# Layer 1 of a two-layer graph network on one core: steps around the norms and the values, paired output tiles, and mask copies on ScalarE

## The chip, the cores and the metric

The kernel runs on one core of a Trainium2 chip. The core has five engines that work side by side, each through its own queue of instructions in order: TensorE (PE, its weight loads shown as PEld), VectorE (DVE), ScalarE (ACT), GpSimd (POOL) and SyncE (SP), which here only issues DMAs. The metric is the time of one execution on the device in microseconds. A profile is one execution recorded instruction by instruction.

## The reference, cut to what matters

There are 32 graphs ("batches") of 512 nodes with 256 features and one 512 x 512 adjacency of zeros and ones each. Two layers follow each other, each with a graph part and a feed-forward part on a layer-normed input, both added to x. The change touches layer 1 alone (besides the adjacency masks of its first batch, which are made while layer 0 still runs).

```python
# layer 1, graph part: 4 heads of 64
h = einsum('bnd,hde->bhne', layernorm(x), W)
weight = mask * (e_src[..., :, None] + e_dst[..., None, :])   # adjacency is 0 or 1
attention = softmax(where(adj == 0, NEG, leaky_relu(weight)))
dst = einsum('bhij,bhje->bhie', attention, h) + bias
out = relu(dst) + h
x = x + (out - mean(out)) / sqrt(var(out) + 1e-6) * gamma + beta      # over each head
# layer 1, feed-forward part: 8 heads of 64, 64 slices
xn = layernorm(x)
fx, xm = xn @ W_fx.T + b_fx, xn @ W_x.T + b_x
sw = softmax((xm @ W_slice.T + b_slice) / temp)                # tokens to slices
st = einsum('bhnc,bhng->bhgc', fx, sw) / (sw.sum(2) + 1e-5)    # slice tokens
ot = hydra(st)            # two-way state-space mixer over the 64 slices
x = x + einsum('bhgc,bhng->bhnc', ot, sw) @ out_w.T + out_b
```

## The kernel before, in words

A batch lies in SBUF as four tiles of 128 nodes (NT = 4) by 256 features. Layer 0 runs first and takes about 2480 us; layer 1 is the generator function `layer1_plain`.

Layer 1 is two streams of Python generators. The stream `attentions` does, batch by batch, `prepare(b)` and `attention(b)`; the preparation of batch b + 1 is interleaved with the attention of batch b by `woven`, in the proportion of `TURNS - 4` to `STEPS`. The stream `mixer(g)` does the feed-forward part for a group of two batches (GB = 2): `slices` for each batch, `tokens`, `scan`, and `unslice` for each batch. Each `yield` in the mixer says how many steps of the attention stream it wants; these are multiplied by `PACE`, which is 1.04 x 2 x (TURNS + STEPS) / WANTED, so that the attention stream runs slightly ahead until `prepare` is stopped by `AHEAD_X = 5` buffers of x. The yields settle only in which order the program is written down: a scheduler then orders the instructions on each engine, with the written order as the priority. So a yield issues nothing by itself.

In `prepare(b)`, POOL gathers the four tiles of x with indirect DMAs (x<-x2s), which need the buffer of batch b - 5 stored. `masks(b)` loads the adjacency (ai), turns it into bf16 with a row sum and a sum of squares on ACT (a, ai), transposes it on PE into a PSUM tile (maskp) of tag "any" and copies that into the uint8 mask. `normed` takes mean and variance on DVE (stc, mvc), the power -0.5 on POOL (`deviation`: an add, then a pow, rsc), the product -mean x power on DVE (shiftc), and the scaling of the four tiles on ACT (hv serves as the buffer). `turned` transposes on PE (x3T). PE then makes hp, ACT takes from it the exponentials and ht, POOL adds the bias (hv<-ht), the source terms go through DRAM to be broadcast to all partitions (own), and DVE multiplies the values hv by their exponentials, one product for each tile.

In `attention(b)`, DVE makes the weights att = max(own, other) x mask for each tile and head, PE multiplies them with hv (avp, two heads side by side) and sums them (adp, four heads side by side). `norm` divides, adds, and normalizes over each head: a sum (mu), the difference, the square on ACT, a second sum, the power on POOL (mu<-mu,eps), and two products on DVE before x gets its sum.

In `slices(b)`, `normed` is used again (std, mvd, rsd, shiftd), the result is transposed (x4T), PE makes the logits of each tile (lgp), ACT the exponentials, DVE multiplies with the bias's exponential, sums, inverts and scales (sw: four operations for each tile), and PE makes yTp from all four tiles and transposes sw (swp). In `unslice(b)`, PE multiplies the transposed weights swT with v into outp and DVE adds each tile to x, which SP then stores.

The PSUM pool has four banks of tag "any"; maskp, x3T, x4T, hp, lgp, yTp, swp, outp and all of the mixer's products take turns in them. The other four banks have the tag "pv" and serve the attention's sums and their transposes.

Of the kernel before, what the change touches and what calls it, by code (L numbers as in the profile page):

```python
# [18 lines left out]
P = 128  # L19
N = 512  # L20
D = 256
NT = N // P
# [4 lines left out]
def deviation(nc, rs, var, eps):  # L27

    nc.gpsimd.tensor_add(rs, var, eps[:, 0:1].to_broadcast(rs.shape))
    nc.gpsimd.tensor_tensor(rs, rs, eps[:, 1:2].to_broadcast(rs.shape), ALU.pow)  # L30
# [819 lines left out]
def layer1_plain(tc, ident, eps, x2s, ranks, adj, w, out, over, ps):  # L850
# [21 lines left out]
    HE = HO + 1  # L872
    AP = AH // 2
    TURNS = AP * NT + 6
    STEPS = 15
    WANTED = 68
    AHEAD = 2
    ATT = 2 * (AHEAD + 2) + AP + 1
    HW = P // AH
# [6 lines left out]
    with ExitStack() as ctx:  # L886
# [11 lines left out]
        def psum(tag, name):  # L898
            return ps.tile([P, N], F32, tag=tag, name=name)
# [158 lines left out]
        def masks(b, bank="any"):  # L1058

            a, raw = [], []  # L1060

            def load(t):
                raw.append(se.tile([P, N], I32, tag="ai", name=f"ai{b}_{t}", bufs=2))
                nc.sync.dma_start(raw[t], adj[b, t * P : (t + 1) * P, :])

            def turn(t):
                pt = ps.tile([P, NT, P], BF16, tag=bank, name=f"maskp{b}_{t}")
                for j in range(NT):
                    nc.tensor.transpose(pt[:, j, :], a[t][:, j * P : (j + 1) * P], identb)
                nc.vector.tensor_copy(mask[:, :, t * P : (t + 1) * P], pt)  # L1070

            load(0)
            load(1)
            yield
            for t in range(NT):
                n = b * NT + t
                a.append(se.tile([P, N], BF16, tag="a", name=f"a{b}_{t}", bufs=3))
                nc.scalar.activation(a[t], raw[t], AF.Identity, accum_out=edges[:, 0, n : n + 1])
                nc.scalar.activation(raw[t], raw[t], AF.Square, accum_out=edges[:, 1, n : n + 1])
                if t + 2 < NT:  # L1080
                    load(t + 2)
                if t == 1:
                    mask = se.tile([P, NT, N], mybir.dt.uint8, tag="mask", name=f"mask{b}")
                    yield
                if t > 1:
                    turn(t - 2)
                    yield
            for t in range(NT - 2, NT):
                turn(t)
                yield  # L1090
            masked[b] = mask
# [11 lines left out]

        xs, ready, attended, stored = {}, {}, set(), set()

        def normed(xt, xn, name):

            mv = sb.tile([P, NT, 2], F32, tag="mv" + name[0], name=f"mv{name}")
            for t in range(NT):
                st = sb.tile([P, 6], F32, tag="st" + name[0], name=f"st{name}_{t}", bufs=4)  # L1110
                nc.vector.bn_stats(st, xt[:, t, :])
                nc.vector.bn_aggr(mv[:, t, :], st)
            rs = sb.tile([P, NT], F32, tag="rs" + name[0], name=f"rs{name}")
            deviation(nc, rs, mv[:, :, 1], eps)
            shift = sb.tile([P, NT], F32, tag="shift" + name[0], name=f"shift{name}")
            nc.vector.scalar_tensor_tensor(shift, mv[:, :, 0], -1.0, rs, ALU.mult, ALU.mult)
            for t in range(NT):
                nc.scalar.activation(xn[:, t, :], xt[:, t, :], AF.Identity, bias=shift[:, t : t + 1],
                                     scale=rs[:, t : t + 1])
# [13 lines left out]
        def prepare(b):  # L1133

            while b >= AHEAD_X and b - AHEAD_X not in stored:
                yield True
            xt = xs[b] = sb.tile([P, NT, D], F32, tag="x", name=f"x{b}", bufs=AHEAD_X)
            for t in range(NT):
                nc.gpsimd.indirect_dma_start(  # L1139
                    out=xt[:, t, :], out_offset=None, in_=x2s[b // SEG],  # L1140
                    in_offset=bass.IndirectOffsetOnAxis(
                        ap=ranks[:, b * NT + t : b * NT + t + 1].bitcast(U32), axis=0))

            hv = sb.tile([P, NT, AH, HE], F32, tag="hv", name=f"hv{b}")
            xn = hv.rearrange("p t h e -> p (t h e)")[:, : NT * D].rearrange("p (t d) -> p t d", t=NT)
            edged = masks(b) if b not in masked else range(3)
            for i, _ in enumerate(edged):
                if i < 3 or b not in masked:
                    yield
                if i == 2:  # L1150
                    normed(xt, xn, f"c{b}")
                    nc.gpsimd.tensor_add(xt, xt, beta.unsqueeze(1).to_broadcast([P, NT, D]))
                    yield
            mask = masked.pop(b)
            xnT = yield from turned(xn, "x3T", f"x3T{b}")
            yield


            ht = sb.tile([P, NT, AH * HO], F32, tag="ht", name=f"ht{b}")
            other = sb.tile([P, NT, AH], F32, tag="other", name=f"other{b}")  # L1160
            mine = sb.tile([P, AH, NT], F32, tag="mine", name=f"mine{b}")
            for t in range(NT):
                ph = psum("any", f"hp{b}_{t}")
                for c in range(DC):
                    nc.tensor.matmul(ph[:, : AH * (HO + 2)], xnT[:, c, t * P : (t + 1) * P], wa[:, c, :],  # L1165
                                     start=c == 0, stop=c == DC - 1)
                d = ph[:, AH * HO : AH * HO + AH]
                nc.scalar.activation(mine[:, :, t], ph[:, AH * (HO + 1) : AH * (HO + 2)], AF.Exp, scale=1.0 - SLOPE)
                nc.scalar.activation(hv[:, t, :, HO], d, AF.Exp)
                nc.scalar.activation(other[:, t, :], d, AF.Exp, scale=SLOPE - 1.0)  # L1170
                nc.scalar.copy(ht[:, t, :], ph[:, : AH * HO])
                yield

            nc.gpsimd.tensor_add(hv[:, :, :, :HO], ht.rearrange("p t (h e) -> p t h e", h=AH),
                                 abias.rearrange("p (h e) -> p h e", h=AH).unsqueeze(1).to_broadcast([P, NT, AH, HO]))
            yield
            pt = psum("any", f"minep{b}")
            nc.tensor.transpose(pt[: AH * NT, :P], mine.rearrange("p h t -> p (h t)"), ident)
            row = sb.tile([AH * NT, P], F32, tag="turned", name=f"turned{b}", bufs=1)
            nc.scalar.copy(row, pt[: AH * NT, :P])  # L1180
            own_row = dr.tile([AH, N], F32, tag="own", name=f"ownd{b}")
            nc.sync.dma_start(own_row.rearrange("h (t p) -> (h t) p", p=P), row)
            own = [wide("own", f"own{b}_{h}", AH + 2) for h in range(AH)]
            for h in range(AH):
                nc.sync.dma_start(own[h], own_row[h].partition_broadcast(P))
            for t in range(NT):
                nc.vector.tensor_mul(hv[:, t, :, :HO], hv[:, t, :, :HO], hv[:, t, :, HO:].to_broadcast([P, AH, HO]))
            ready[b] = mask, ht, hv, other, own
            yield
# [112 lines left out]
        def slices(b, j, yT, rn):  # L1302
# [3 lines left out]
                next(ahead)  # L1306
            xt = xs[b]
            xn = sb.tile([P, NT, D], F32, tag="xn", name=f"x4{b}", bufs=1)
            normed(xt, xn, f"d{b}")
            yield 5  # L1310
            xnT = yield from turned(xn, "x4T", f"x4T{b}", 1)
            nc.gpsimd.tensor_add(xt, xt, outb.unsqueeze(1).to_broadcast([P, NT, D]))
            sw = sb.tile([P, NT, DI], F32, tag="sw", name=f"sw{b}", bufs=1)
# [231 lines left out]

        def unslice(b, swT, v):
            xt = xs.pop(b)
            for t in range(NT):
                po = psum("any", f"outp{b}_{t}")
                for k in range(KC):  # L1550
                    nc.tensor.matmul(po[:, :D], swT[:, k, t * P : (t + 1) * P], v[:, k, :],  # L1551
                                     start=k == 0, stop=k == KC - 1)
                nc.vector.tensor_add(xt[:, t, :], xt[:, t, :], po[:, :D])
            nc.sync.dma_start(out[b].rearrange("(t p) d -> p t d", p=P), xt)
            stored.add(b)

        def mixer(g):
            uT = sb.tile([P, KC, GB * G], F32, tag="uT", name=f"uT{g}", bufs=1)
            yT = sb.tile([P, DC, H, GB, G], F32, tag="yT", name=f"yT{g}", bufs=1)
            rn = sb.tile([P, GB, KC], F32, tag="rn", name=f"rn{g}")  # L1560
            sws = []
            for j in range(GB):
                sws.append((yield from slices(g * GB + j, j, yT, rn)))
            yield 3
            tokens(g, yT, rn, uT)
            v = yield from scan(g, uT)
            yield 2
            for j in range(GB):
                unslice(g * GB + j, sws[j], v[:, j])
                yield 2  # L1570


# [651 lines left out]
```

## Time and profile before

| | |
|---|---|
| median of 3 runs | 4619.16 us (4616.48 to 4621.86) |
| the profiled execution's own time | 4623.49 us |
| its span, first to last instruction | 4621.6 us |
| granted PE clock in it | 0.951 |
| PE busy | 4067.9 us |
| DVE busy | 3379.1 us |
| ACT busy | 2291.7 us |
| POOL busy | 1729.5 us |
| DMA | 474.09 MB moved |

The page and the trace give busy time by engine, groups of instructions by line and tile with their mean duration, the idle time ahead of each group with what ended it, and an account of who waited for whom. In a group's row, "x128" is the count; after the bar stand the total busy time in us and the mean of one in ns; after the second bar the idle time of that engine just before these instructions, and the releasers. In a timeline the columns are start in us, duration in us, engine, line, operation, tiles, count, and in brackets the idle time before it with what ended it. In the account of waits a row gives the total in us, the number of times and the longest. A matmul of f32 operands stands in the trace as two instructions.

### The profile page before, as it was taken

The numbers are of one execution on the slowest core, as the hardware profiler recorded it, in microseconds if no ns is written. First come the engines' busy times: TensorE is split into PE (matmuls) and PEld (weight loads), VectorE is DVE, ScalarE is ACT, GpSimd is POOL, SyncE is SP. The second block draws the span as 40 slices with busy tenths as digits, with TensorE's granted clock in tenths as the row PEclk, the third lists the DMA queues.
The fourth block names the chain that finished last, engine by engine and source line by source line (L and its number), as shares of the span: only waits on it lengthen the run. The fifth ranks groups of instructions, "written<-read, shape, count | busy, mean of one in ns | idle before, by whom it ended". The sixth has DMA issues, their size and how long they took to land. (4 is left out here: it accounts for less than half of the span.)

```text
span 4621.6 us, 56127 instructions
## 1 busy us (share of the span) xinstructions
PE 4067.9 (88%) x19287; PEld 2525.4 (55%) x19287; DVE 3379.1 (73%) x7040; ACT 2291.7 (50%) x4756; POOL 1729.5 (37%) x2027
## 2 busy tenths in 40 slices
PE   5768898988988889888897899999999999999987
PEld 4545655656556566555554355555555555555555
DVE  6678778887788877777775777777787777777763
ACT  2344555545655556555564444545544454454432
POOL 2356444653435534353332223222323323332220
PEclk8889999999999999998998999999999999999998
DMA  5556433653436533374431111111111111111100
GB/s 125 172 158 214 164 127 126 198 178 124 136 118 198 177 129 112 99 263 145 141 115 48 53 46 56 51 48 44 44 54 49 56 56 53 47 54 56 40 14 15
DMA packets 235100, 474.09 MB, mean 103 GB/s; under 512 B 38299, under 2 KB 114075, under 8 KB 234804
## 3 DMA queue, kind: packets, MB, share of 16 engines
q0 software_dynamic: 80256, 282.38, 19.3%
q1 hardware_dynamic: 154548, 188.02, 13.3%
q8 instruction: 154, 2.52, 0.2%
q14 instruction: 142, 1.16, 0.1%
HBM read 413.16 MB, written 57.16 MB: 102 GB/s over the span
## 5 line engine op out<-in xcount | busy, mean ns | idle before, releaser
L609 PE MATMUL clsp<-xnT,wc 128*128 128x512 f32 x1024 | 512.1, 621 | 77.3 <-ACT cls L611 63.0
L609 PE MATMUL gatep<-xnT,wg 128*128 128x512 f32 x1024 | 497.7, 605 | 16.0 <-ACT gate L611 13.2
L638 PE MATMUL po<-wd,acc 128*128 128x256 f32 x2048 | 450.9, 381 | 0.4 <-DVE acc L627 0.3
L638 PEld LDWEIGHTS po<-wd,acc 128*128 128x128 f32 x2048 | 391.4, 191 | 65.9 <-issue 13.8
L422 PE MATMUL pm<-h,adj 128*128 128x257 f32 x1024 | 295.5, 435 | 136.3 <-DVE xs L640 67.3
L589 DVE SCALAR_TENSOR_TENSOR best<-rows,xs,best 128x1024 f32<-128x1024 f32 x212 | 276.1, 1305 | 165.4 <-ACT best L583 98.1
L623 DVE SCALAR_TENSOR_TENSOR acc<-past,fld,acc 128x512 f32<-128x512 f32 x448 | 351.1, 787 | 54.3 <-ACT past L622 45.5
L1198 DVE SCALAR_TENSOR_TENSOR att<-own,other,mask 128x512 f32<-128x512 f32 x512 | 378.9, 762 | 11.5 <-DMA own<-ownd 11.0
L586 POOL DMA_INDIRECT rows<-table,xs x212 | 261.1, 1232 | 237.3 <-DVE best L589 171.8
L609 PEld LDWEIGHTS gatep<-xnT,wg 128*128 128x128 f32 x1024 | 195.8, 195 | 260.5 <-issue 197.0
L622 ACT ACTIVATE past<-tz,fld 128x512 f32<-128x512 f32 x448 | 291.0, 694 | 83.4 <-DVE acc L623 83.0
L618 ACT ACTIVATE acc<-tz,fld 128x512 f32<-128x512 f32 x256 | 199.5, 779 | 265.1 <-PE tz L616 262.0
L422 PEld LDWEIGHTS pm<-h,adj 128*128 128x128 f32 x1024 | 212.4, 218 | 194.5 <-issue 106.7
L1231 PE MATMUL avp<-att,hv 128*64 128x512 f32 x1024 | 310.3, 628 | 4.2 <-DVE att L1198 4.2
L609 PEld LDWEIGHTS clsp<-xnT,wc 128*128 128x128 f32 x1024 | 185.7, 197 | 222.3 <-issue 121.1
L1331 PE MATMUL yTp<-sw,x 128*128 128x512 f32 x512 | 242.7, 614 | 39.8 <-DVE sw L1326 32.3
L611 ACT ACTIVATE cls<-clsp,fld 128x512 f32<-128x512 f32 x256 | 176.7, 690 | 201.7 <-PE clsp L609 86.9
L1319 PE MATMUL lgp<-wsl,x4T 128*128 128x512 f32 x512 | 252.0, 628 | 27.9 <-DVE mask L1070 21.7
L1139 POOL DMA_INDIRECT x<-x2s,ranks x128 | 140.9, 1101 | 343.0 <-DVE att L1198 104.1
L1284 POOL TENSOR_TENSOR mu<-mu,eps 128x16 f32<-128x16 f32 x32 | 121.3, 3791 | 324.2 <-DVE mu L1283 323.1
L611 ACT ACTIVATE gate<-gatep,fld 128x512 f32<-128x512 f32 x256 | 175.6, 686 | 127.5 <-PE gatep L609 103.6
L541 POOL DMA_INDIRECT xs<-rows_of,order x128 | 143.4, 1121 | 250.7 <-DVE acc L623 78.7
(597 smaller groups left out, 8961.5 us busy)
## 6 DMA issues: line engine op xcount, KB each, us to landing
adji<-in_adj SPq DMA_DIRECT2D x128, 256.0 KB
ai<-in_adj SPq DMA_DIRECT2D x128, 256.0 KB
own<-ownd SPq DMA_DIRECT2D x128, 256.0 KB
rows_of<-keep SPq DMA_DIRECT2D x32, 550.0 KB
x<-in_x SPq DMA_DIRECT2D x32, 512.0 KB
x2s<-xs SPq DMA_DIRECT2D x32, 512.0 KB
out<-x SPq DMA_DIRECT2D x32, 512.0 KB
rows<-table,xs POOLq DMA_INDIRECT x212
```

The source lines that it names most:

```text
L422: nc.tensor.matmul(pm[:, : D + 1], a[:, i, t * P : (t + 1) * P], h[:, i, :], start=i == 0, stop=i == NT - 1)
L586: nc.gpsimd.indirect_dma_start(out=row, out_offset=None, in_=table, in_offset=bass.IndirectOffsetOnAxis(ap=idxs[:, k : k + 1].bitcast(U32) ...
L589: nc.vector.scalar_tensor_tensor(m, row, vals[:, k : k + 1], m, ALU.add, ALU.max)
L609: nc.tensor.matmul(pf, wf[:, c, f * P : (f + 1) * P], xnT[:, c, :], start=c == 0, stop=c == DC - 1)
L611: nc.scalar.activation(o, pf, fn, bias=fld[:, f, bf : bf + 1], scale=1.0 if fn == AF.Gelu else 0.5)
L622: nc.scalar.activation(r, z, AF.Relu, bias=fld[:, f, AT + b : AT + b + 1])
L623: nc.vector.scalar_tensor_tensor(y, r, fld[:, f, CH + b : CH + b + 1], y, ALU.mult, ALU.add)
L638: nc.tensor.matmul(po[:, i, :], acc[f][:, t * P : (t + 1) * P], wd[:, f, :], start=f == 0, stop=f == FC - 1)
L1198: nc.vector.scalar_tensor_tensor(e, own[h], other[:, j, h : h + 1], mask[:, j, :], ALU.max, ALU.mult)
L1231: nc.tensor.matmul(pv[q][k * HO : (k + 1) * HO, :], hv[:, j, h, :HO], weighed[b, h, j], start=j == 0, stop=j == NT - 1)
L1319: nc.tensor.matmul(pf, xnT[:, c, t * P : (t + 1) * P], wsl[:, c, :], start=c == 0, stop=c == DC - 1)
L1331: nc.tensor.matmul(py, xn[:, t, c * P : (c + 1) * P], sw[:, t, :], start=t == 0, stop=t == NT - 1)
```

## The change

Five edits, all in `layer1_plain`:

- In `masks`, the copy of maskp into the mask is issued on ACT instead of DVE. There are 128 of them, 4 for each batch.
- `normed` becomes a generator and yields once between the power on POOL and the product that uses it. In `prepare` it also starts after the fourth step of `masks` instead of the third; in `slices` the yield of 5 that followed it is split into 2 inside and 3 after.
- `prepare` yields once more between the row of `own` (and the bias added on POOL) and the products of hv.
- `unslice` puts two output tiles into one PSUM bank, adds both with one DVE instruction, and yields 1 after the first pair.
- `STEPS` and `WANTED`, which set the pace, follow: 15 to 17 and 68 to 70.

```diff
-    STEPS = 15
-    WANTED = 68
+    STEPS = 17
+    WANTED = 70
...
-                nc.vector.tensor_copy(mask[:, :, t * P : (t + 1) * P], pt)
+                nc.scalar.copy(mask[:, :, t * P : (t + 1) * P], pt)
...
-        def normed(xt, xn, name):
+        def normed(xt, xn, name, want=None):
...
             deviation(nc, rs, mv[:, :, 1], eps)
+            yield want
             shift = sb.tile([P, NT], F32, tag="shift" + name[0], name=f"shift{name}")
             nc.vector.scalar_tensor_tensor(shift, mv[:, :, 0], -1.0, rs, ALU.mult, ALU.mult)
...
-            edged = masks(b) if b not in masked else range(3)
+            edged = masks(b) if b not in masked else range(4)
             for i, _ in enumerate(edged):
-                if i < 3 or b not in masked:
-                    yield
-                if i == 2:
-                    normed(xt, xn, f"c{b}")
+                yield
+                if i == 3:
+                    yield from normed(xt, xn, f"c{b}")
                     nc.gpsimd.tensor_add(xt, xt, beta.unsqueeze(1).to_broadcast([P, NT, D]))
                     yield
...
                 nc.sync.dma_start(own[h], own_row[h].partition_broadcast(P))
+            yield
             for t in range(NT):
                 nc.vector.tensor_mul(hv[:, t, :, :HO], hv[:, t, :, :HO], hv[:, t, :, HO:].to_broadcast([P, AH, HO]))
...
-            normed(xt, xn, f"d{b}")
-            yield 5
+            yield from normed(xt, xn, f"d{b}", 2)
+            yield 3
...
         def unslice(b, swT, v):
             xt = xs.pop(b)
-            for t in range(NT):
-                po = psum("any", f"outp{b}_{t}")
-                for k in range(KC):
-                    nc.tensor.matmul(po[:, :D], swT[:, k, t * P : (t + 1) * P], v[:, k, :],
-                                     start=k == 0, stop=k == KC - 1)
-                nc.vector.tensor_add(xt[:, t, :], xt[:, t, :], po[:, :D])
+            for t0 in range(0, NT, 2):
+                po = psum("any", f"outp{b}_{t0}").rearrange("p (t d) -> p t d", t=2)
+                for i in range(2):
+                    t = t0 + i
+                    for k in range(KC):
+                        nc.tensor.matmul(po[:, i, :], swT[:, k, t * P : (t + 1) * P], v[:, k, :],
+                                         start=k == 0, stop=k == KC - 1)
+                nc.vector.tensor_add(xt[:, t0 : t0 + 2, :], xt[:, t0 : t0 + 2, :], po)
+                if t0 == 0:
+                    yield 1
             nc.sync.dma_start(out[b].rearrange("(t p) d -> p t d", p=P), xt)
...
-                unslice(g * GB + j, sws[j], v[:, j])
+                yield from unslice(g * GB + j, sws[j], v[:, j])
```

## The prediction

> **What bounds the kernel now.** I read the engine shares first, then busy time in stretches, then who TensorE (PE) waited for, then the group rows of what is edited, then the timeline of the stretch where the masks are made.
>
> ```profile
> PE 4067.9 (88%) x19287; PEld 2525.4 (55%) x19287; DVE 3379.1 (73%) x7040; ACT 2291.7 (50%) x4756; POOL 1729.5 (37%) x2027
> ```
>
> PE is the busiest, DVE comes second, ACT has half its time free. All edits but four mask copies lie in layer 1, from about 2480 us on. One stretch of its steady part, busy us by engine:
>
> ```profile
> 3200.00:3600.00 400.00, 375.98 (x2261) 219.32 (x2260) 293.27 (x624) 200.93 (x522) 119.67 (x90) 0.98 0.17 50
> ```
>
> PE 94%, DVE 73%, ACT 50%, DMA 0.17: PE's own work sets the pace, and only its idle 6% can be won or doubled. From 2800 to 4400 us that is 97 us, 7.5 us for each group of two batches (a group takes 126 us). PE's waits from 2700 to 4500 us (total, times, longest):
>
> ```profile
> PE yTp L1331 <- DVE sw L1326: 32.3, 26, 1.8
> PE lgp L1319 <- DVE mask L1070: 21.7, 6, 4.4
> PE maskp L1069 <- DVE mask L1070: 12.4, 7, 3.0
> PE oTp L1519 <- ACT yT L1513: 12.2, 15, 1.3
> PE yTp L1511 <- DVE y L1506: 11.5, 9, 4.8
> PE yp L1496 <- DVE mix L1489: 11.2, 5, 6.9
> ```
>
> Two sorts stand out: the slice weights sw (data), and the mask copies (a PSUM bank of tag "any" that DVE has not emptied): 34.1 us, plus 0.8 in smaller rows. How a mask wait arises, at 3250 us:
>
> ```profile
> 3250.76 1.05 POOL L30 TENSOR_TENSOR rsc<-rsc,eps 128x4 f32<-128x4 f32 x1
> 3251.84 0.16 DVE L1116 SCALAR_TENSOR_TENSOR shiftc<-mvc,rsc 128x4 f32<-128x4 f32 x1 [2.27 <-POOL rsc L30]
> 3251.91 0.68 DVE L1321 TENSOR_TENSOR sw<-sw,ebsl 128x512 f32<-128x512 f32 x1
> ...
> 3252.52 0.68 DVE L1070 CAST mask<-maskp 128x512 uint8<-128x512 bf16 x1
> ...
> 3253.26 1.22 PE L1319 MATMUL lgp<-wsl,x4T 128*128 128x512 f32 x1 [3.09 <-DVE mask L1070]
> ```
>
> POOL's power is late, DVE stands at the shift, the mask copy queues behind it, PE has no bank. The mask is the messenger; the norm's power is the cause.
>
> [...]
>
> ```profile
> L1070 DVE CAST mask<-maskp 128x512 uint8<-128x512 bf16 x108 | 73.2, 678 | 3.1 <-PE maskp L1069 3.1
> L1332 ACT COPY yT<-yTp 128x512 f32<-128x512 f32 x56 | 32.8, 586 | 211.0 <-PE yTp L1331 211.0
> L1553 DVE TENSOR_TENSOR x<-x,outp 128x256 f32<-128x256 f32 x115 | 47.6, 414 | 98.9 <-PE outp L1551 98.8
> L1259 DVE TENSOR_TENSOR av<-bp,rs 128x512 f32<-128x512 f32 x58 | 37.8, 677 | 0.1
> ```
>
> **The change, part by part.** Where instructions land I take from the order in which the two built programs stand on each engine; a scheduler makes it, and it holds no times.
>
> *Masks on ACT.* 128 copies x 0.68 = 87 us leave DVE; 128 x 0.59 = 75 us come to ACT (no copy of bf16 to uint8 on ACT is in the trace[...]; I take 0.59). Table loads stay equal in number. ACT goes from 50% to 51%. What queues behind the copies: in each group's first half ACT now stands as Square of the attention norm, mask, a, mask, ai, both x4T copies, four hv scalings, then the exps. In before two groups of three have x4T ahead of that Square. The Square waits for DVE's av minus mean (3746.0 in the group of 3729.5). From there: 1.0 + two masks 1.2 + a and ai with their accumulator reads 1.6 + x4T 0.6 gives x4T at about 3751.8 (av is 1.4 us later in the new order), where PE, by the pieces that stand ahead of lgp, is ready at about 3749.9: a new wait of some 2 us, if nothing later in that half ends later anyway.
>
> *Pairs of outputs.* 128 adds x 0.414 = 53 us become 64 x 0.68 (row L1259) = 44 us on DVE; the matmuls stay 1024. Half the bank turns. The adds now stand behind six att products instead of alternating with them, but own arrives earlier (its transpose stands ahead of oTp), so the output DMA and the gathers behind it on POOL start within some 2 us of before. At the very end the last add is 0.26 us longer. Nothing counted.
>
> *Steps between power and use.* These waits stand on DVE:
>
> ```profile
> DVE hv L1187 <- POOL hv L1174: 111.1, 28, 8.2
> DVE shiftc L1116 <- POOL rsc L30: 52.0, 27, 3.3
> DVE shiftd L1116 <- POOL rsd L30: 37.7, 29, 1.4
> ```
>
> The step issues nothing; it would pay if other DVE work came between. In the new order it does not: between the last statistics and shift stand 0 or 1 instructions in the steady groups (before 0 to 4), and the four hv products still follow a shift with at most two tiny operations between. So of these 201 us I count nothing won. What does move is on POOL: rsc stands behind four gathers instead of six or seven in two groups of three, and the attention norm's power (mu) between gathers one and two of the second batch. DVE's product with mu moves from behind the first half's sw chain to ahead of it. Price, with the group of 3729.5, whose order is nearest:
>
> ```profile
> 3753.26 0.16 DVE L1116 SCALAR_TENSOR_TENSOR shiftc<-mvc,rsc 128x4 f32<-128x4 f32 x1 [1.22 <-POOL rsc L30]
> ...
> 3767.29 0.68 DVE L1326 TENSOR_TENSOR sw<-sw,sst 128x512 f32<-128x512 f32 x1
> ```
>
> ```profile
> 3755.71 3.17 POOL L1284 TENSOR_TENSOR mu<-mu,eps 128x16 f32<-128x16 f32 x1
> ```
>
> After the change, from the shift on: gather 1.3 and power 3.2 end at +4.6; DVE has 1.5 us of att to fill that, so it stands still for some 3 us. Then av 1.1, att 0.7, x 1.1, twelve sw operations at their pitch of 0.60 and 0.5 of reciprocals: sw of tile 2 at +14.8, tile 3 at +15.4 (before +14.7). PE then has six yTp of 0.87 left: swp at +20.0, before 18.3; but PE has by then done the first hp (0.9), so +0.8 us. This group was the best pattern: between first outp and first swp PE idles 2.8 us there and 4.0 in the mean of groups 0 to 12. Against the mean: -0.4 us. The x4T wait lies ahead of sw and is inside this. Had no sw delay arisen, -2.7 (all mask waits); had PE caught the whole stall, +3.
>
> *Second half.* Four att products come between the sw operations (4 x 0.66), covered by dp and bp (2.6 us) that move ahead of yTp; the adT copy can come behind a later exp: +0.5 us, between -1 and +1.5.
>
> *Splits.* Pairs of avp and quads of adp that overlap on PE are broken up 51 times before and 48 after: nothing.
>
> *Start and pacing.* PE waited 9.3 us for x3T1 on a mask copy behind shifts; the copies gone, DVE starts batch 0's products some 2.5 us sooner: -3 us (0 to -9). STEPS and WANTED scale together: a group earns 64.5 steps for the 62 it needs, before 60.3 for 58, the same lead of 4%.
>
> *Sum.* 14 groups x (-0.4 + 0.5) = +1; start -3; and since each hand-run wait counts only what I saw queue, I add 0.5 us a group for in-order waits I did not: +7. Total +5 on the profiled execution (span 4621.6, own time 4623.5): 4628.5; that run lies 4.3 us over the median of the runs shown, so 4624.
>
> **Rivals.** A measurement of this kernel tells some 0.2% (9 us) from no change.
>
> *Waits change names (0.42).* As summed: 4624, own range 4608 to 4640. For it: PE is 94% busy, and the sw chain ends just when PE needs it.
>
> *The power becomes DVE's stall (0.28).* POOL's mu power stands behind a gather that waits for the output store; DVE stops at av ahead of the sw chain. It decides once the stall exceeds the 2 us that the freed copies and earlier rsc give. Exposed at 2 us in 14 groups: +28, 4647; with the x4T wait on top 4675. For it: PE already waits on sw in 26 places. Against: the power is 3.2 us and POOL is free when it is due.
>
> *Mask waits truly go (0.30).* ACT empties banks at once, DVE's freed 97 us bring sw forward: -2 us x 14 - 3 = -31, 4588. For it: ACT is half idle and mostly waits for PE (211 us before yT alone). Against: x4T now queues behind those copies.
>
> *The steps do nothing.* That is inside all three: the shift waits stay.
>
> **Numbers.** Time 4624. Range 4585 to 4668: the mask case down to full removal (-35), the stall at 3 us in 14 groups (+42) with the 7 us of unseen waits. Faster: nearly all of the third case and 0.04 of the first, 0.32; same 0.20; slower 0.48.
>
> **What would show it.** Right: mask rows on ACT near 590 ns; PE waits ended by a mask under 10 us; shift waits still 70 to 110 us; new DVE waits of av on POOL mu in each group's first half; PE waits for x4T on ACT and for sw on DVE up. Wrong: shift waits halved; PE idle in a group under 6 us (then 4590) or over 9.5 us (then 4655).

## The result, and the profile after

The changed kernel took 4632.16 us in the median of 8 runs (4625.41 to 4639.29), the kernel before 4622.19 us in 8 runs beside it (4607.51 to 4635.2): a ratio of 1.0029, 95% interval 1.0011 to 1.0048. It is slower by 0.3%. The profiled execution has a span of 4637.0 us and an own time of 4638.72 us.

The engine shares (first line of the page) and the steady stretch (busy time in a window; after the busy times of PE, PEld, DVE, ACT and POOL come the granted clock, the DMA share and GB/s):

```profile
PE 4060.0 (88%) x19287; PEld 2519.9 (54%) x19287; DVE 3306.3 (71%) x6848; ACT 2351.8 (51%) x4884; POOL 1746.4 (38%) x2027
```

```profile
3200.00:3600.00 400.00, 370.44 (x2208) 218.23 (x2207) 275.45 (x571) 204.43 (x525) 122.06 (x87) 0.98 0.17 52
```

DVE's busy time fell by 73 us and ACT's grew by 60. In this stretch DVE fell from 293 to 275 us, yet PE fell too, from 376.0 to 370.4 of 400 us: relief on DVE did not reach PE. Whom PE waited for from 2700 to 4500 us (total in us, times, longest):

```profile
PE yTp L1332 <- DVE sw L1327: 58.1, 40, 2.8
PE yTp L1512 <- DVE y L1507: 35.1, 14, 4.8
PE lgp L1320 <- ACT x4T L1129: 9.6, 12, 1.5
```

No wait on a mask is left (34 us before). In its place the waits for the slice weights sw went from 32.3 to 58.1 us, for the scan's y from 11.5 to 35.1, for x4T from 0.4 to 9.6. DVE's own waits in the same stretch:

```profile
DVE av L1288 <- POOL mu L1285: 71.6, 27, 7.4
...
DVE shiftc L1117 <- POOL rsc L30: 38.1, 27, 4.1
DVE shiftd L1117 <- POOL rsd L30: 36.6, 28, 1.4
```

The two shift waits came to 74.7 us (89.7 before); the wait of av on the power mu went from 24.7 to 71.6. The moved and paired instructions (groups by shape):

```profile
L1070 ACT CAST mask<-maskp 128x512 uint8<-128x512 bf16 x128 | 72.8, 578 | 17.2 <-PE maskp L1069 17.1
L1556 DVE TENSOR_TENSOR x<-x,outp 128x512 f32<-128x512 f32 x64 | 43.8, 684 | 82.6 <-PE outp L1554 82.6
```

**Where the 15.4 us of the two profiles lie.** Cut at the first xp matmul of each group, the time up to the first group fell by 9.7 us (2674.2 to 2664.5), the 14 steady groups grew by 25.7 (1769.9 to 1795.7), and the tail fell by 0.6. PE's idle time in the 14 groups grew by 17.6 us. The other 8 us are put down to TensorE's clock. The trace records what was granted; in the 14 steady groups it is either 1.00 or 0.50. The time at 0.50, called half clock here, grew from 51.2 to 78.5 us. Half of PE's busy time in it is counted as lost work: 32.3 us instead of 24.0, so 8.3 more. That half is an estimate from the granted share, and a high one: in the changed kernel's steady groups a matmul of oTp took 0.43 us in the mean at half clock and 0.28 at full, one of yTp from sw 1.08 and 0.60, so 1.6 and 1.8 times as long. The experiments use this account, in us over the 14 steady groups of each profile. "Lost" is half of PE's busy time at half clock; the remainder is steady time less idle less lost, so by that estimate PE's work as if at full clock.

| kernel | ratio to before (95%) | steady | PE idle | half clock | lost | remainder |
|---|---|---|---|---|---|---|
| before | 1 | 1769.9 | 107.2 | 51.2 | 24.0 | 1639 |
| changed | 1.0029 (1.0011-1.0048) | 1795.7 | 124.8 | 78.5 | 32.3 | 1639 |
| 1 masks | 0.9966 (0.9950-0.9982) | 1758.8 | 103.9 | 41.0 | 18.6 | 1636 |
| 2 pairs | 1.0095 (1.0080-1.0110) | 1814.3 | 109.2 | 116.0 | 55.0 | 1650 |
| 3 steps | 1.0080 (1.0067-1.0093) | 1806.3 | 134.2 | 85.3 | 34.9 | 1637 |
| 4 masks, pairs | 0.9888 (0.9874-0.9903) | 1726.5 | 82.7 | 30.7 | 13.9 | 1630 |
| 5 changed, small out_b sum | 0.9964 (0.9950-0.9977) | 1753.2 | 97.2 | 34.1 | 15.9 | 1640 |
| 6 changed, both sums small | 0.9955 (0.9942-0.9969) | 1763.1 | 100.0 | 51.2 | 23.1 | 1640 |
| 7 masks, pairs, attention step | 0.9899 (0.9884-0.9914) | 1725.6 | 77.7 | 23.9 | 11.1 | 1637 |
| 8 masks, pairs, slices' step | 0.9910 (0.9895-0.9925) | 1729.5 | 80.7 | 34.1 | 16.1 | 1633 |
| 9 masks, pairs, values' step | 0.9961 (0.9947-0.9975) | 1758.4 | 105.0 | 41.0 | 19.2 | 1634 |
| 10 changed, no values' step | 0.9908 (0.9893-0.9923) | 1738.9 | 82.0 | 41.0 | 19.0 | 1638 |
| 11 changed, wait filled | 1.0033 (1.0021-1.0045) | 1798.9 | 109.6 | 58.0 | 26.5 | 1663 |
| 12 changed, short power | 0.9979 (0.9968-0.9990) | 1770.7 | 104.0 | 61.4 | 28.0 | 1639 |

Kernel 11 has some 24 us of added matmuls in its remainder. All the others lie within 1630 to 1650 us: what sets the versions apart is mostly how long PE stands, and how long it works at half clock. Each row but for its ratio is one profiled execution, which lay up to 6.6 us from its kernel's median; the ratios are the firmer numbers.

### The profile page after: what moved, and what is told of

It reads as the page before. It is cut to its first block, busy times and chain, and to the rows that moved or that the text cites. A ratio compares the mean times of both kernels' runs of the same rounds, so it can differ in the third digit from the quotient of the medians.

```text
span 4637.0 us, 55996 instructions
## 1 busy us (share of the span) xinstructions
PE 4060.0 (88%) x19287; PEld 2519.9 (54%) x19287; DVE 3306.3 (71%) x6848; ACT 2351.8 (51%) x4884; POOL 1746.4 (38%) x2027
## 3 DMA queue, kind: packets, MB, share of 16 engines
q0 software_dynamic: 80256, 282.38, 19.2%
## 4 chain that ended last, share of the span: by engine, by line
PE 39%; DVE 23%; POOL 10%; issue 9%; DMA 9%; ACT 5%; SPq 0%; POOLq 0%; DVEq 0%; ACTq 0%
PE avp L1232 4%; PE clsp L609 3%; PE gatep L609 3%; PE yTp L1332 3%; DMA rows<-table,xs 3%; DVE acc L623 3%; PE outp L1554 3%; PE adp L1239 2%; DVE att L1199 2%; PE hp L1165 2%; PE pm L422 2%; DMA rows<-table,tops 2%; DVE best L589 2%; PE oTp L1520 2%; PE po L638 2%
## 5 line engine op out<-in xcount | busy, mean ns | idle before, releaser
L609 PE MATMUL gatep<-xnT,wg 128*128 128x512 f32 x1024 | 498.7, 606 | 17.6 <-ACT gate L611 15.0
L622 ACT ACTIVATE past<-tz,fld 128x512 f32<-128x512 f32 x448 | 291.2, 694 | 81.6 <-DVE acc L623 81.1
L1320 PE MATMUL lgp<-wsl,x4T 128*128 128x512 f32 x512 | 243.1, 612 | 12.4 <-ACT x4T L1129 11.8
L625 DVE TENSOR_TENSOR acc<-acc,cls 128x512 f32<-128x512 f32 x256 | 188.1, 736 | 59.4 <-ACT acc L618 55.9
```

Source lines behind the costliest of these rows:

```text
L609: nc.tensor.matmul(pf, wf[:, c, f * P : (f + 1) * P], xnT[:, c, :], start=c == 0, stop=c == DC - 1)
L622: nc.scalar.activation(r, z, AF.Relu, bias=fld[:, f, AT + b : AT + b + 1])
L1320: nc.tensor.matmul(pf, xnT[:, c, t * P : (t + 1) * P], wsl[:, c, :], start=c == 0, stop=c == DC - 1)
```

## The experiments

### The parts by themselves

**1, masks on ScalarE alone**

```diff
-                nc.vector.tensor_copy(mask[:, :, t * P : (t + 1) * P], pt)
+                nc.scalar.copy(mask[:, :, t * P : (t + 1) * P], pt)
```

> The kernel before with the mask copies on ScalarE alone. Theory 'the start gains, the steady groups lose by the steps': the wait of x3T1 on a mask copy at the start of layer 1 goes (9.3 us in the profile before), PE waits ended by a mask (34 us) go, other in-order waits take most of their place; total -9 us, range -20 to 0, x3T1 start gain of 7 to 10 us seen here already. Rival 'ScalarE's copies delay x4T': PE waits for x4T near 10 us and a total of 0 to +10 us.

Measured: 0.9966, some 16 us faster. PE's waits on masks were gone, those on sw rose to 60.1 us, as the theory said; those on x4T were 1.4 us, not 10, so the rival fell. At the start, PE's wait of x3T1 (9.3 us before) was 0; it is 9.0 and 9.6 us in the next two kernels, whose masks stay on DVE.

**2, pairs alone**

```diff
-            for t in range(NT):
+            for t0 in range(0, NT, 2):
...
-                nc.vector.tensor_add(xt[:, t, :], xt[:, t, :], po[:, :D])
+                nc.vector.tensor_add(xt[:, t0 : t0 + 2, :], xt[:, t0 : t0 + 2, :], po)
+                if t0 == 0:
+                    yield 1
```

> The kernel before with outputs in pairs alone (their step between the two pairs included). Theory: nothing, 0 +- 9 us; PE waits of yTp on y near 12 us as before. Rival 'pairs are the cause of the slower groups' (the adds stand later on DVE, so the store and the next gathers come later, and POOL's sums move against DVE's y): +15 to +30 us, with waits of yTp on y near 35 us.

Measured: 1.0095, 44 us slower. The theory (nothing) is wrong, and so is the rival's mechanism: y waits were 1.9 us. DVE's waits for own were 81.1 us (11.0 before), but version 4 has 73.5 of them and is the fastest, and PE's idle time hardly grew. By the account 31 us are lost clock (half-clock time 116.0 against 51.2 us), 11 the remainder. Of the 116 us, 44 follow waits of 1.4 to 1.6 us of PE for x3T from ACT (12.3 us in all, 5.7 before): PE hardly stands longer, but in pieces that have half clock behind them (see 11). Why the pairs alone move these waits was not tried.

**3, steps alone**

```diff
-    STEPS = 15
+    STEPS = 17
...
             deviation(nc, rs, mv[:, :, 1], eps)
+            yield want
...
                 nc.sync.dma_start(own[h], own_row[h].partition_broadcast(P))
+            yield
```

> The kernel before with the new steps alone (between power and use in both norms, ahead of the values' products, two steps more for the preparation). Theory 'the steps lose': they move DVE's product with mu ahead of sw (waits av on POOL mu over 50 us) and shift POOL's sums onto DVE's y (waits of yTp on y over 25 us): +15 to +30 us. Rival 'the steps do nothing': 0 +- 9 us, waits of the shifts still 70 to 110 us in both theories.

Measured: 1.0080, 37 us slower. The steps do cost, against the rival: waits of av on mu were 59.8 us. But y waits stayed at 12.4; PE lost instead 23.1 us to the exponentials of the logits and 16.6 to the sums sst. The mechanism is half of what was named. In this kernel the masks stay on DVE, and PE's waits on them stay too.

**4, masks and pairs without the steps**

The edits of 1 and 2 together.

> Masks on ScalarE and outputs in pairs, without the new steps. Theory 'the steps lose': start gain of 9 us kept, steady groups as before: -9 us (-20 to 0). Rival 'pairs lose' or 'the loss belongs to any changed order': +5 to +25 us, waits of yTp on y over 25 us.

Measured: 0.9888, 52 us faster, at 4564.73 us: the best version seen, faster than both kernels. It is beyond the range that the theory gave; the rival fell. Pairs cost 44 us alone and, on top of the masks' change, win 36. The parts don't add; in this version the waits for x3T are back at 5.2 us and the half-clock time at 30.7. Adding the steps turns 52 us won into 13 lost.

### What the steps do to PE

**5, a small out_b sum.** In the changed kernel eight of the 14 steady groups, every second one but for the last, had their y late. The timeline of such a group, DVE, then POOL, then PE:

```profile
3201.76 1.95 DVE L1505 TENSOR_TENSOR y<-xk,dq 128x512 f32<-128x512 f32 x1
...
3204.46 2.62 DVE L1507 TENSOR_TENSOR y<-y,z 128x512 f32<-128x512 f32 x1
```

```profile
3200.80 2.36 POOL L1313 TENSOR_TENSOR x<-x,outb 128x1024 f32<-128x1024 f32 x1 [6.74 <-ACT x L1119]
3204.19 2.34 POOL L1174 TENSOR_TENSOR hv<-ht,abias 128x1024 f32<-128x1024 f32 x1 [1.03 <-ACT ht L1171]
```

```profile
3207.13 1.12 PE L1512 MATMUL yTp<-ident,y 128*128 128x128 f32 x4 [3.80 <-DVE y L1507]
3208.04 0.42 PE L1178 MATMUL minep<-ident,mine 128*16 128x128 f32 x1
3208.93 5.85 PE L1520 MATMUL oTp<-yT,hoT 128*128 128x128 f32 x32 [0.46 <-ACT yT L1514]
```

In the other six groups these two y operations take 0.69 us. Here the first ends at 3203.71 and POOL's first sum at 3203.16; the last ends at 3207.08, POOL's second sum at 3206.53. Both end 0.55 us after POOL's instruction, which had started first both times; of an operation that takes 0.69 us elsewhere, most would then have run once POOL was done. Not every DVE instruction beside such a sum is stretched: in the profile before, while POOL's sum of x and beta ran (3761.43 to 3763.81 us), a mask copy at 3761.70 took its usual 0.68 us and an sw operation at 3762.41 took 1.96. The mechanism was not shown.

```diff
-            nc.gpsimd.tensor_add(xt, xt, outb.unsqueeze(1).to_broadcast([P, NT, D]))
+            nc.gpsimd.tensor_add(xt[:, :, :8], xt[:, :, :8], outb[:, :8].unsqueeze(1).to_broadcast([P, NT, 8]))
```

> The changed kernel with GpSimd's sum of x and out_b cut to 8 of each tile's 256 columns (the rest of that bias is left out of the output); the instructions stand in the same order on every engine. Theory 'GpSimd's sums stretch DVE's y, PE stands still for 3.8 us and its clock is then halved': the first y operation of the slow groups takes 0.7 us and not 1.95, the wait of yTp on y falls from 3.8 to some 2.5 us, fewer half-clock stretches in the 14 steady groups (78 us of half clock now, then 30 to 50), total 15 to 35 us under the changed kernel. Rival 'y is late because what feeds it is late': y waits stay near 35 us, total within 9 us of the changed kernel.

Measured: 0.9964, so 0.65% under the changed kernel, some 30 us. Every y operation of the layer took 0.68 or 0.69 us, and PE's wait was 0.62 us in each of the 14 groups. PE's waits in this kernel:

```profile
PE yTp L1332 <- DVE sw L1327: 55.3, 38, 2.4
PE yTp L1512 <- DVE y L1507: 12.9, 14, 4.8
```

The waits on sw stayed near 58 us: this cause is separate from theirs. The theory held, and the wait fell further than it said: the second operation was expected to stay late, but once the first was on time, the last ended before POOL's sum of the values began (3186.84 and 3187.14 us in the same group).

**6, both sums small**

```diff
-            nc.gpsimd.tensor_add(hv[:, :, :, :HO], ht.rearrange("p t (h e) -> p t h e", h=AH),
...
+            nc.gpsimd.tensor_add(hv[:, 0, :, :HO], ht[:, 0].rearrange("p (h e) -> p h e", h=AH),
...
+                nc.vector.tensor_mul(hv[:, t, :, :HO], hv[:, t, :, :HO] if t == 0 else ht[:, t].rearrange("p (h e) -> p h e", h=AH),
```

> As the kernel with the small out_b sum, and GpSimd's sum of the values and their bias is cut to one of four tiles (the bias is left out of the other three; DVE's products take ht there). Theory: no y operation over 1 us, waits of yTp on y at 10 to 15 us, half clock under 45 us, total 30 to 50 us under the changed kernel; DVE's wait of hv on POOL falls too, but PE doesn't stand for it. Rival: y waits stay near 35 us, gain under 10 us.

Measured: 0.9955, the same as the last within the intervals: nothing more to be had from the second sum, for the reason just given. DVE's wait of hv on POOL fell from 112.7 to 51.7 us and bought nothing.

**11, PE's wait filled.** Of the 78.5 us of half-clock time in the changed kernel, 51 stand at y. Stretches of the group above (columns as before), then two of 3.41 us that end and begin where the clock changes:

```profile
3200.00:3205.00 5.00, 3.33 (x24) 2.65 (x22) 3.34 (x4) 2.97 (x14) 3.16 (x2) 1.00 0.09 12
3205.00:3210.00 5.00, 2.40 (x10) 1.91 (x11) 3.42 (x5) 1.45 (x4) 1.53 (x1) 0.64 0.13 43
3210.00:3215.00 5.00, 5.00 (x37) 4.88 (x36) 0.00 (x0) 0.18 (x1) 0.00 (x0) 0.68 0.57 180
```

```profile
3202.94:3206.35 3.41, 0.39 (x2) 0.00 (x0) 3.34 (x3) 1.18 (x7) 2.38 (x2) 1.00 0.31 79
3206.35:3209.77 3.42, 2.17 (x9) 1.68 (x10) 2.07 (x5) 1.45 (x4) 0.18 (x1) 0.50 0.00 0
```

At 3206.4 us the clock halves (1.00 to 0.50), during the wait of 3.80 us, and is full again 6.8 us later; the 32 matmuls oTp take 5.85 us, against 3.84 in the group at 3336. All eight waits of y that last 3.8 us in the steady groups have such a stretch, which begins between 1.7 us before and 0.6 us after their end; none of the six of 0.62 us has.

```diff
             pt = psum("any", f"yTp{g}")
+            for k in range(16):
+                nc.tensor.transpose(pt[:, k % KC * P : (k % KC + 1) * P], xk[:, k % KC * P : (k % KC + 1) * P], ident)
```

> The changed kernel with 16 needless transposes of xk (16 x 0.11 = 1.8 us) on TensorE between hp and the transposes of y, into the bank that those overwrite; the order on the other engines is the same, so DVE's y stays stretched to 1.95 and 2.6 us. Theory 'an idle of 3.8 us halves the clock for some 7 us and that costs PE about 3 us each time': the half-clock stretches behind y go (from 78 us to under 45 us of half clock in the steady groups), so some 17 to 25 us come back, and in the groups whose wait was 0.6 us the fill costs up to 1.2 us (6 groups, 7 us): total -5 to -20 us against the changed kernel although more work is done. Rival 'the idle itself is the whole cost, the clock does not matter': +5 to +12 us against the changed kernel.

Measured: 1.0033 against 1.0029, no difference that the intervals tell. Neither the theory's gain nor the rival's loss came. The wait shrank to 2.07 us, but six of the eight still had a half-clock stretch behind them, now 3.4 us each, where seven of eight had 6.8. By the account idle fell by 15.2 us and lost clock by 5.8, which the fill (24 us more in the remainder) used up. In this profile the shorter wait cost less clock; that 2.07 us is short enough is refuted.

The traces show what went before the half clock. In the steady groups of all 14 profiles the clock changes only on marks 3.413 us apart, which lie differently in each execution; in the kernel before and the changed one the stretches at half clock there last one or two such steps (3.41 or 6.83 us). Cut at the marks, a stretch at full clock with 2.0 us or more of PE idle was followed by one at half clock in 92 of 92 cases, one with less than 1.7 us in 11 of 6782, and one between these in 51 of 119. So in these profiles it is the sum of PE's idle time between two marks that counts. Of the eight waits of 2.07 us, six left 2.06 us or more of idle in one stretch; the two without half clock were divided by a mark, and their stretches had at most 1.35 and 1.96 us of it. A wait of 3.8 us has at least 1.9 us on one side of a mark wherever it falls (2.1 or more in these eight).

**12, a short power.** The second wait that grew is that on sw. In the changed kernel DVE's product of av with mu stands ahead of the four sw chains in 13 of the first 14 groups; in the kernel before, and in 2, 4 and 8, it is behind at least 14 of their 16 operations in every one of the 14. DVE's timeline of a group of the changed kernel, then of a group of kernel 10 with the product behind, each from the shift:

```profile
3367.46 0.16 DVE L1117 SCALAR_TENSOR_TENSOR shiftc<-mvc,rsc 128x4 f32<-128x4 f32 x1 [1.21 <-POOL rsc L30]
...
3371.84 1.23 DVE L1288 TENSOR_TENSOR av<-av,mu 128x1024 f32<-128x1024 f32 x1 [2.82 <-POOL mu L1285]
...
3374.78 1.29 DVE L1322 TENSOR_TENSOR sw<-sw,ebsl 128x512 f32<-128x512 f32 x2
...
3377.42 3.07 DVE L1327 TENSOR_TENSOR sw<-sw,sst 128x512 f32<-128x512 f32 x2
```

```profile
3347.51 0.15 DVE L1117 SCALAR_TENSOR_TENSOR shiftc<-mvc,rsc 128x4 f32<-128x4 f32 x1
...
3348.24 1.32 DVE L1321 TENSOR_TENSOR sw<-sw,ebsl 128x512 f32<-128x512 f32 x2
...
3357.79 1.21 DVE L1287 TENSOR_TENSOR av<-av,mu 128x1024 f32<-128x1024 f32 x1
```

The sw chains begin 7.3 us after the shift in the one and 0.7 in the other.

```diff
-            nc.gpsimd.tensor_tensor(mu[:, 1, :], mu[:, 1, :], eps[:, 1:2].to_broadcast([P, NG]), ALU.pow)
+            nc.gpsimd.tensor_tensor(mu[:, 1, :AH], mu[:, 1, :AH], eps[:, 1:2].to_broadcast([P, AH]), ALU.pow)
```

> The changed kernel with GpSimd's power of the attention norm (mu) on 4 of its 16 columns (the power is left out of the other 12); the order on every engine is the same. Theory 'in the changed order DVE stands at the product with mu ahead of the slice weights, and PE waits for sw': the power takes 1.0 us and not 3.2, DVE's waits of av on POOL mu fall from 72 us to under 30, PE's waits of yTp on sw from 58 to under 35, total 15 to 35 us under the changed kernel (4597 to 4617). Rival 'sw ends no earlier, since the exponentials of the logits end last': waits of sw on ACT's exponentials rise by what the waits on mu fall, total within 9 us of the changed kernel.

Measured: 0.9979, 0.50% under the changed kernel, some 23 us. The stall in that order fell from 2.8 to 0.9 us in most groups (DVE's waits of av from 71.6 to 21.5 us), and PE's waits on sw to 40.5, above the 35 expected; y waits stayed at 35.1. DVE's waits of sw on the exponentials rose by 3 us alone, so the rival fell. The stall is one cause of the waits on sw and not the only one: kernel 1 has 60.1 us of them with the product ahead, or all but ahead, in four groups of 14, kernel 10 has 30.5 with it so in eight.

Experiments 5 and 12 take two separate causes out. In the steady groups of these profiles they are worth 42.5 and 25.0 us, and 1795.7 less both is 1728, next to 1726.5 in the version without steps. But the profiled execution of the changed kernel lay 6.6 us above its median and that of kernel 5 lay 5.9 below, so the first is overstated by some 12 us. By the medians the two are worth 30 and 23 of the 65 us that the steps cost. Both were not taken out in one kernel; if they add, they are some four fifths of the price, and the rest is open.

### Which step it is

Kernels 7, 8 and 9 add one of the three steps to version 4; kernel 10 takes one from the changed kernel. `STEPS` follows: 16 in 7, 9 and 10, 15 in 8.

**7, the step in the attention's norm** (and its statistics one step later):

```diff
-            edged = masks(b) if b not in masked else range(3)
+            edged = masks(b) if b not in masked else range(4)
...
+                    yield from normed(xt, xn, f"c{b}")
```

> Masks on ScalarE and pairs (4565 us) plus the step in the attention's norm alone (its statistics one step later, and a step between power and shift). Theory 'any step moves GpSimd's sums and the power of mu against DVE's order, and it is luck where they fall': +20 to +60 us, the extra being PE idle plus half of the half-clock time. Rival 'this step is harmless, the other two do it': 0 +- 9 us.

Measured: 0.9899, the same as without it (0.9888). The rival held.

**8, the step in the slices' norm**

```diff
-            normed(xt, xn, f"d{b}")
-            yield 5
+            yield from normed(xt, xn, f"d{b}", 2)
+            yield 3
```

> Masks on ScalarE and pairs (4565 us) plus the step in the slices' norm alone (two of its five wanted steps between power and shift). Theory 'this step brings x4T, and with it GpSimd's sum of x and out_b, against y': +20 to +60 us with waits of yTp on y over 25 us. Rival 'harmless': 0 +- 9 us, y waits near 12 us as without it.

Measured: 0.9910, with y waits of 11.6 us: harmless within the intervals.

**9, the step ahead of the values' products alone**

```diff
                 nc.sync.dma_start(own[h], own_row[h].partition_broadcast(P))
+            yield
```

> Masks on ScalarE and pairs (4565 us) plus the step ahead of the values' products alone. Theory 'this step is the one that costs': y waits of PE over 25 us, three or more half-clock stretches behind waits of yTp of some 3.8 us, total +40 to +70 us, near the changed kernel (4632). Rival 'only the three steps together cost': 0 to +15 us, y waits near 12 us.

Measured: 0.9961, some 0.7% or 34 us above version 4. PE's waits on sw rose from 29.1 to 55.4 us; the product with mu now stood ahead of sw, or among its operations, in 13 of 14 groups. But no y operation was stretched, and y waits were 12.9. So this step costs, and the longer waits are at the sw chain; the collision at y came only with the others too. Neither the theory nor its rival had it so.

**10, the changed kernel without that step**

```diff
                 nc.sync.dma_start(own[h], own_row[h].partition_broadcast(P))
-            yield
```

> The changed kernel without the step ahead of the values' products (masks, pairs and the two norms' steps stay). Theory 'that step costs': 4565 +- 12 us, y waits near 12 us, half clock near 30 us in the steady groups. Rival 'the steps add up': 4590 to 4635 us.

Measured: 0.9908, 4574.27 us, with y waits of 13.5 and sw waits of 30.5 us. The theory held in the time and the y waits (half clock was 41.0 us, not 30): taking this one step out wins 1.2% (1.0029 to 0.9908). It does not bring the old order back: mu's product is still ahead of the sw chain, or behind its first operation alone, in 8 of 14 groups. Why the scheduler orders so was not tried.

## Why the prediction was right, point by point

The forecast was 4624 us on a median of 4619 (a ratio of 1.001), with slower by over 0.2% the likeliest at 0.48; measured was 1.0029, inside the range of 4585 to 4668 us. The direction and the signs were right. That the size came out so near is in part luck: the sum has a few us of small terms where the runs show two large ones that nearly cancel, a gain of 52 us by masks and pairs and a loss of 65 by the steps.

- **What would show it.** All the signs came: mask rows of 578 ns on ACT (forecast 590, an estimate next to the 586 of yT's copy), no PE wait ended by a mask (under 10 us), shift waits of 74.7 us (70 to 110), new waits of av on mu, PE's waits for x4T and sw up, 8.9 us of PE idle in a group (between 6 and 9.5). "Waits change names" is what happened, with the mechanism of its first rival, the power that becomes DVE's stall, as one of the new waits.
- **The mu stall** was sized some 3 us; 2.82 in the group shown. Shortening it won 23 us in experiment 12, so that rival's mechanism was real, with others beside it. The last sw product was placed 15.4 us after the shift and ended at 16.8 us: the pair at 3377.42 took 3.07 us where 1.28 is usual, while POOL's sum of x and beta ran (3376.97 to 3379.33), as at y. The profile before has this too: in the group that the prediction reads, the sw operation at 3762.41 took 1.96 us and ended 0.56 us after the same sum of POOL's. **First half** (first outp to first swp): -0.4 us a group forecast, -0.1 measured (4.05 to 3.98 us of idle). **Second half** (swp to swp): +0.5 forecast, +0.3 measured (1.18 to 1.49 us).
- **Start**: -3 us forecast, with a bound at -9. The wait of 9.3 us vanished; from the first x3T0 to the first xp the profile fell by 7.7 us (159.6 to 151.9), so as a term of the sum it was mis-sized by a factor of two and a half. But not all of this need be the wait: kernel 3, which still has a wait of 9.6 us there, took 154.0 us. The other 2 us of the 9.7 lie ahead of x3T0, whose start scatters from 2504.7 to 2514.6 us over the profiles.
- **Unseen in-order waits**, the term put at +0.5 us a group, +7 in all, was the one most under-sized. The stretch from xp to the next outp, which the sum had nothing for, went from 2.2 to 3.3 us of idle a group, +16 in all, by POOL's sums against y; and the clock, by the account's estimate, took 8.3 more. The prediction read DVE's and POOL's queues apart and gave a DVE operation one duration, whatever POOL did; and it gave TensorE one clock. In the profile before, 37.5 of the 51.2 us at half clock follow stretches in which PE waited longest for a mask, so the mask waits seem to have cost clock beyond the 34 us that it counted.
- **"Nothing" for the steps and the pairs** failed. The steps win nothing at the shifts, as said. But they cost 37 us alone and 65 in company (4 against the changed kernel), the pairs cost 44 alone and win 36 with the masks.
- **The rival "mask waits truly go"** (4588) did not come true for this change, but not for the reason held against it: the waits for x4T cost 9.6 us and no more. Without the steps it does come true, and further, at 4565.

## What to carry to other kernels

Where PE is 94% busy, count a wait twice: for its length, and for the clock that it may cost after it. Here half clock came in 92 of 92 cases where PE's idle time added up to 2.0 us or more between two of the marks 3.413 us apart; look at the granted clock around the longest waits. A step that issues nothing is not free when a scheduler sets the order: look at which instruction each queue now has ahead of the one that PE waits for, and at which of POOL's sums run beside DVE's work on the path (here y took 2.62 us instead of 0.69). Run the parts of a change singly and in pairs; here a version 1.2% faster was in the diff all along, with one yield left out (and STEPS at 16).

## What the runs showed of the hardware that was not expected

- Two 128x512 f32 operations of y on DVE took 1.95 and 2.62 us instead of 0.69 beside POOL's 128x1024 sums, and ended 0.55 us after them.
- In the steady groups of the 14 profiles TensorE's clock changed only on marks 3.413 us apart. After 2.0 us or more of PE idle between two marks it was halved in 92 of 92 cases, after less than 1.7 us in 11 of 6782. So waits for y of 3.8 us were followed by half clock for 3.4 or 6.8 us eight times in eight, those of 2.07 us for 3.4 us six times in eight, those of 0.62 us never. The 32 matmuls oTp behind one wait of 3.8 us took 5.85 us instead of 3.84.
- POOL's power on 128x4 instead of 128x16 elements took 1.86 us in the mean against 3.75, not a quarter.
